# Layer 1's self-attention in a two-layer decoder: values projected by tiles of 128 tokens and moved to batches by DMAs, loads of expert results tied to the steps

## The chip, the cores and the metric

The kernel runs on one core of a Trainium2 chip. A core has five engines with a queue of instructions each: TensorE (PE in the profile, its weight loads PEld), VectorE (DVE), ScalarE (ACT), GpSimd (POOL) and SyncE (SP), which here only issues DMAs. Each queue is worked off in its order. An instruction that needs the result of another queue, or a buffer that another queue still reads, waits at the head of its own queue, and what stands behind it waits too. Matrix products go to PSUM, in eight banks of 128 partitions x 512 floats; the other data lie in SBUF or, outside the core, in HBM. The metric is the time of one execution on the device in microseconds (us).

## What is computed

Two decoder layers over 32 sequences of 100 tokens with 256 features, all in float32. Each layer adds three parts to x, each of the normed x: self-attention, attention to a context of 361 tokens, and a mixture of experts. The part that matters here is the self-attention of layer 1, which has no softmax: scores under the causal mask are used as they are.

```python
def _layernorm(x, axis=-1, eps=1e-05):
    m = jnp.mean(x, axis=axis, keepdims=True)
    v = jnp.var(x, axis=axis, keepdims=True)
    return (x - m) / jnp.sqrt(v + eps)

def _L1_attn_ref(x, W1, b1, W2, b2):
    bs, t, d = x.shape          # 32, 100, 256
    h = N_HEADS                 # 16 heads of 16
    kqv = x @ W1 + b1
    k, q, v = jnp.split(kqv, 3, axis=-1)
    k, q, v = (to_heads(k), to_heads(q), to_heads(v))
    mask = jnp.tril(jnp.ones((t, t), dtype=bool))
    attn = jnp.where(mask, jnp.einsum('bhqd,bhkd->bhqk', q, k), 0.0)
    out = jnp.einsum('bhqk,bhkd->bhqd', attn, v)
    out = out.transpose(0, 2, 1, 3).reshape(bs, t, d)
    return out @ W2 + b2

x = x + _L0_ffn_ref(_layernorm(x), ...)      # two of eight experts for each token
x = x + _L1_attn_ref(_layernorm(x), L1_attn_W1, L1_attn_b1, L1_attn_W2, L1_attn_b2)
x = x + _L1_xattn_ref(_layernorm(x), ctx_512, ...)
```

## The kernel before

x stays in SBUF for the whole program as 25 tiles of 128 tokens (`self.x`, tile f holds tokens 128f to 128f+127 of the 3200), and so does its normed transpose `xnT`. A batch is a sequence of 100 tokens, so a tile cuts across batches: `pieces(b)` lists the parts of tiles that make up batch b, `tile_of(b)` names the tile that batch b completes (or none). The stages follow each other; the one that the change touches is `l1_attn` (1612 to 1785 us of the profiled span), between layer 0's experts (`l0_ffn`) and layer 1's attention to the context.

Layer 0's experts leave their results in HBM (`y_d`), two rows for each token. `gather0(pool, f)` brings them home for tile f: SyncE loads both rows of 128 tokens (L1275, 256 KB, into `yk`, of which there are six buffers), and VectorE adds each, times its weight, to x (L1280, two instructions). After it `norm_stats(f, ...)` takes the mean and variance of the tile on VectorE (L198, L201), and for a group of three tiles (four in the first) the root on ScalarE and its reciprocal. `turn` normalizes the rows of a group (L210), transposes them on TensorE (L232) and copies them to `xnT` (L151 on ScalarE, L152 on VectorE).

The loop runs over steps b = 0 to 33. Step b holds, in the order in which TensorE has it (the order of TensorE is the program's, under `manual_schedule`):

- `scores(b)`: 32 small matmuls for the 16 heads of batch b into four PSUM banks; VectorE multiplies each bank by the mask into SBUF (L1010, four instructions).
- `proj`: queries or keys for one half of the features of the four batches after the present four (four matmuls of 400 columns), to SBUF by ScalarE (L978, L981).
- `vals(b + 1)`: the values of the next batch, four matmuls of 100 tokens x 256 features; VectorE adds the bias into one of three tiles `v0` to `v2` (L991, two instructions). The tiles have 32 columns for each head and hold zeros in the half that the head does not use (even heads use the first 16, odd ones the second), cleared once.
- `values(b - 1)`: 32 small matmuls of masked scores and values (L1020), copied by ScalarE into the transposed tile `zT` (L1027).
- `out(b - 2)`: where that batch completes a tile, the output projection (L157 with `zT`), which VectorE adds to x (L262), and the statistics for the next layer part's norm.
- where there are batches eight ahead: in steps with i = b % 4 < 3 the gather and statistics of one tile of the group two ahead, in the step with i = 3 the turn of that group.
- at times, norm rows and transposes for the next part (GpSimd L210, L1045).

On the other engines the order is made by a scheduler at build time, from the program's order, its own estimate of durations, and dependences; `depend(a, [b], ...)` adds one. In `gather0`, `after` sets VectorE's additions behind the last normalized row. On SyncE the 25 loads `yk` stand in one row, with nothing of this stage between them; a load waits only for its buffer, that is for the additions of the tile six before it.

All tiles of PSUM in this stage share one tag with eight banks, handed out in turn, so the next step's scores need the banks of the present step's scores back.

Of the kernel before, what the change touches and what calls it, by code (L numbers as in the profile page):

```python
# [9 lines left out]
F32 = mybir.dt.float32  # L10
# [3 lines left out]
ALU = mybir.AluOpType  # L14
AX = mybir.AxisListType

P = 128
NB = 32
T = 100
NT = NB * T  # L20
NF = NT // P
D = 256
NK = D // P
H = 16
# [55 lines left out]
def tiles_before(n):  # L80

    return n * T // P


def tile_of(b):

    f = tiles_before(b + 1)
    return f - 1 if f > tiles_before(b) else None


def pieces(b):

    t = 0
    while t < T:
        f, o = divmod(b * T + t, P)
        n = min(P - o, T - t)
        yield f, slice(o, o + n), slice(t, t + n)
        t += n


class Kernel:
# [825 lines left out]
    def l1_attn(self):  # L927
        nc, tc, a = self.nc, self.tc, self.a
        with ExitStack() as st:
            self.psum = st.enter_context(self.banks("l1a", t=8))  # L930
            wk, wq, wv, wo, bqk, bv, bo, xbo = self.w1a
            cp = st.enter_context(tc.tile_pool(name="c1a", bufs=1))
            pool = st.enter_context(tc.tile_pool(name="p1a", bufs=2))
# [7 lines left out]
            at = cp.tile([P, 1], F32, tag="at", name="at")  # L941
# [5 lines left out]
            for j in range(2):  # L947
                got = nc.vector.tensor_scalar(bias[:, j, :], bqk[:, 0, :], own[:, j : j + 1], None, ALU.mult)
                self.depend(got, [self.late.ins], "behind the last block")
            got = nc.vector.tensor_copy(bias[:, 2, :], bqk[:, 2, :])  # L950
            self.depend(got, [self.late.ins], "behind the last block")
            vs = [cp.tile([T, H, 32], F32, tag=f"v{i}", name=f"v{i}") for i in range(3)]
            for v in vs:
                nc.gpsimd.memset(v, 0.0)
            q, k, s, later = {}, {}, {}, deque()
            self.z_begin(pool, 2)

            def group(i):

                f = (0, 3 * i + 1)[i > 0]  # L960
                return range(f, f + FRONT1[f])

            def turn(f, n):
                self.norm_turn(f, n, self.norm_rows(f, n, bias=bo), self.bank_m())

            def proj(b0, i):

                c, of_k = divmod(i, 2)
                if c == 0:
                    if of_k:  # L970
                        k[b0 // 4] = pool.tile([P, 2, 4 * T], F32, tag="kT", name="kT")
                    else:
                        q[b0 // 4] = pool.tile([P, 2, 2, 4 * T], F32, tag="qT", name="qT")
                pm = self.bank_m()[:, : 4 * T]
                w = wk if of_k else wq
                self.mm(pm, [(w[:, i, c * P : (c + 1) * P], self.xn_of(i, b0, 4)) for i in range(NK)])
                if of_k:
                    nc.scalar.activation(k[b0 // 4][:, c, :], pm, AF.Identity, bias=bias[:, 2, c : c + 1])  # L978
                else:
                    for j in range(2):  # L980
                        nc.scalar.activation(  # L981
                            q[b0 // 4][:, c, j, :], pm, AF.Identity, bias=bias[:, j, c : c + 1], scale=own[:, j : j + 1]
                        )

            def vals(b):
                pm = self.bank_m()[:T, :D]
                self.mm(pm, [(self.xn_of(i, b), wv[:, i, :]) for i in range(NK)])
                pv, pb = (t.rearrange("p (h j d) -> p h j d", j=2, d=16) for t in (pm, bv[:T, :]))
                v = vs[b % 3].rearrange("p (h j) e -> p h j e", j=2)
                for j in range(2):  # L990
                    nc.vector.tensor_tensor(  # L991
                        v[:, :, j, 16 * j : 16 * j + 16], pv[:, :, j, :], pb[:, :, j, :], ALU.add
                    )

            def rows_of(r):
                return slice(32 * r, 32 * r + 32)
# [18 lines left out]
            def values(b):  # L1015
                pz = self.bank_z()[:, : 2 * T].rearrange("p (c t) -> p c t", c=2)
                for c in range(2):
                    for j in range(2):
                        for r in range(4):
                            nc.tensor.matmul(  # L1020
                                pz[rows_of(r), c, :], lhsT=vs[b % 3][:, 8 * c + 2 * r + j, :],
                                rhs=s[b, r][:, c, j, :], start=(j == 0), stop=(j == 1),
                            )
                for r in range(4):
                    del s[b, r]
                for z, cols in self.z_parts(b):
                    nc.scalar.copy(z, pz[:, :, cols])  # L1027

            def out(b):

                f = tile_of(b)
                if f is None:
                    return
                self.out_proj(f, wo)
                self.norm_stats(f, HALVES)
                if f in (5, 11, 17):
                    waiting.extend(range(f - 5, f, 2))
# [9 lines left out]

            waiting = deque()


            self.ahead_of = 1

            def ahead(n):
                self.turn_wk1()
                done = []
                for i in range(n):
                    b, half = divmod(i, 2)
                    for c in range(NKC):
                        done.append(self.vals1(b, half, c))
                return done[2 * len(done) // 3]  # L1060

            with tc.manual_schedule(engines={mybir.EngineType.PE}):
                for i in range(2):
                    for f in group(i):
                        if i > 0:
                            self.gather0(pool, f, self.last_row)
                            self.norm_stats(f, FRONT1)
                    if i == 0:
                        self.norm_after = ahead(AHEAD)
                        for f in group(0):  # L1070
                            self.norm_stats(f, FRONT1)
                        self.norm_after = None
                    f = group(i)[0]
                    turn(f, 2)
                    turn(f + 2, len(group(i)) - 2)
                    if i == 0:
                        for c in range(4):
                            proj(0, c)
                vals(0)
                for b in range(NB + 2):  # L1080
                    i = b % 4
                    b0 = b - i
                    if b < NB:
                        scores(b)
                    if b0 + 4 < NB:
                        proj(b0 + 4, i)
                    if b + 1 < NB:
                        vals(b + 1)
                    if 0 < b <= NB:
                        values(b - 1)  # L1090
                    if b > 1:
                        out(b - 2)
                    if b0 + 8 < NB:
                        fs = group(b0 // 4 + 2)
                        if i < 3:
                            self.gather0(pool, fs[i], self.last_row)
                            self.norm_stats(fs[i], FRONT1)
                        else:
                            turn(fs[0], 2)
                            turn(fs[2], 1)  # L1100
                    if later:
                        later.popleft()()
                    if waiting:
                        next_norm()
                while later:
                    later.popleft()()
# [160 lines left out]
                got = nc.sync.dma_start(word, self.y_d[0:1, 0:1])  # L1267
                self.depend(got, [more.ins], "the blocks' results")

    def gather0(self, pool, f, after=None):  # L1270

        nc = self.nc
        pr2 = self.picked0
        y2 = pool.tile([P, 2, D], F32, tag="yk", name="yk", bufs=6)
        got = nc.sync.dma_start(y2, self.y_d.rearrange("(k f p) d -> f p k d", k=2, p=P)[f])  # L1275
        self.depend(got, [self.y_done.ins], "the blocks' results")
        self.tc.declare_no_dep(got.ins, group="y0b", reason="SyncE has waited in the branch")
        for k in range(2):
            y = y2[:, k, :]
            got = nc.vector.scalar_tensor_tensor(  # L1280
                self.x[:, f, :], y, pr2[:, k, f : f + 1], self.x[:, f, :], ALU.mult, ALU.add
            )
            if after is not None:
                self.depend(got, [after.ins], "not ahead of the first tiles' norm")
# [842 lines left out]
```

## Time and profile before

| what | us |
|---|---|
| three timed runs | 2978.18, 2972.26, 2978.78 (median 2978.18) |
| profiled execution | 2953.32 |
| its span, first to last instruction | 2951.6 |
| granted TensorE clock over the span | 0.986 |
| the changed stage in it | about 1612 to 1785 |
| TensorE busy in 1711 to 1785 | 73.85 of 74.00 |
| wait of the loads `yk` for VectorE's additions (their buffers) | 60.9 in 10 waits, longest 19.0 |

A row of the page or of the windows gives busy microseconds and, after an x, instructions. A row of the timeline gives the start, the length, the engine, the line of the kernel, the operation, the tile written and the tiles read, the shapes (partitions x elements), and how many like instructions are merged in it. A float32 product shows as two instructions, so the two halves of a contraction over 256 features make four. Of matmuls in a row, the distance from one start to the next tells more than the length, since they overlap.

### The profile page before, as it was taken

To read this page: it belongs to the slowest core of one execution; us is meant where nothing else is said; L and a number is where in the kernel's file an instruction comes from. 1 tells how busy PE (TensorE), PEld (TensorE's weight loads), DVE (VectorE), ACT (ScalarE), POOL (GpSimd) and SP (SyncE) were. 2 spreads that over 40 slices of the span, in tenths; PEclk is the share of its full clock that TensorE was granted. 3 is DMA by queue.
4 is the path that set the end of the run, shared out by engine and by line. 5 is a ranking of instruction groups with operands and counts; after the bars stand their busy time and mean duration, and the time that the engine had idled before them with its cause. 6 is when DMAs were issued, how large, how long until landed. Compare 5 with 4: busy or idle time off the path is not lost. (4 is left out here: it accounts for less than half of the span.)

```text
span 2951.6 us, 66511 instructions
## 1 busy us (share of the span) xinstructions
PE 2843.2 (96%) x26012; PEld 2165.8 (73%) x26012; DVE 1786.2 (61%) x5119; ACT 1412.2 (48%) x4261; POOL 922.3 (31%) x1081
## 2 busy tenths in 40 slices
PE   8999999999999999999999999999999999999992
PEld 6777777677777766888886667777777777776672
DVE  6665666577777762222225878676676676776553
ACT  5555555467666641222223224565566565667220
POOL 3222221266666536222222230011311212123364
PEclk9999999999999989999999999999999999999997
DMA  8870000000000004565553100010000000000396
GB/s 316 280 263 1 1 1 1 12 15 16 16 16 16 10 28 144 196 221 176 199 214 131 34 2 10 6 42 20 26 12 12 12 12 11 13 10 5 109 214 190
DMA packets 126198, 222.37 MB, mean 75 GB/s; under 512 B 39434, under 2 KB 104645, under 8 KB 119088
## 3 DMA queue, kind: packets, MB, share of 16 engines
q1 hardware_dynamic: 95808, 123.87, 13.1%
q0 software_dynamic: 26784, 90.83, 9.5%
q8 instruction: 210, 3.44, 0.5%
q10 hardware_dynamic: 3280, 3.28, 0.3%
q14 instruction: 116, 0.95, 0.1%
HBM read 152.12 MB, written 111.18 MB: 89 GB/s over the span
## 5 line engine op out<-in xcount | busy, mean ns | idle before, releaser
L1723 POOL DMA_INDIRECT x_d<-xr,slot x200 | 195.2, 976 | 676.4 <-ACT eT L791 548.2
L157 PE MATMUL ps_t<-xnT,wA 128*128 128x200 f32 (+1 forms) x1608 | 329.3, 348 | 0.8 <-DVE x_sb L262 0.6
L157 PE MATMUL ps_t<-cT,q 128*128 128x361 f32 x832 | 317.3, 470 | 0.0
L791 ACT COPY eT<-ps_t 124x384 f32<-124x384 f32 (+1 forms) x416 | 193.6, 473 | 224.6 <-PE ps_t L790 224.3
L781 ACT ACTIVATE wBx<-ps_t,m 128x361 f32<-128x361 f32 x416 | 235.8, 568 | 121.7 <-DVE m L778 117.6
L157 PEld LDWEIGHTS ps_t<-xnT,wA 128*128 128x128 f32 x1608 | 270.2, 190 | 32.0 <-issue 13.2
L540 DVE TENSOR_REDUCE m<-ps_t 100x1 f32<-100x361 f32 x512 | 239.5, 524 | 46.5 <-PE ps_t L157 46.3
L157 PE MATMUL ps_t<-xT,w 128*128 128x256 f32 (+1 forms) x1276 | 260.2, 363 | 0.7 <-ACT xT L151 0.7
L778 DVE TENSOR_REDUCE m<-ps_t 128x1 f32<-128x361 f32 x416 | 218.3, 526 | 60.4 <-PE ps_t L157 58.4
L157 PEld LDWEIGHTS ps_t<-xT,w 128*128 128x128 f32 x1276 | 223.6, 190 | 36.2 <-issue 9.3
L790 PEld LDWEIGHTS ps_t<-ident,wBx 128*124 128x124 f32 x1248 | 156.1, 139 | 123.5 <-issue 68.2
L359 POOL TENSOR_TENSOR e<-e,rz 100x400 f32<-100x400 f32 x128 | 109.3, 854 | 406.4 <-DVE rz L358 402.3
L562 ACT ACTIVATE e<-ps_t 121x300 f32<-121x300 f32 x512 | 173.9, 426 | 119.2 <-PE ps_t L157 119.2
L790 PE MATMUL ps_t<-ident,wBx 128*124 128x128 f32 x1248 | 204.0, 275 | 5.3 <-DVE m L1659 2.1
L355 ACT ACTIVATE e<-s,m 100x100 f32<-100x100 f32 x512 | 186.1, 365 | 20.8 <-DVE m L349 20.1
L157 PE MATMUL ps_t<-wA,cT 128*124 128x512 f32 x384 | 193.9, 592 | 0.0
L783 DVE TENSOR_SCALAR wBx<-wBx,sums 128x361 f32<-128x361 f32 x416 | 173.3, 417 | 9.9
L1377 DVE TENSOR_TENSOR h<-ps_t,g 128x256 f32<-128x256 f32 (+1 forms) x145 | 58.2, 401 | 188.5 <-ACT g L1376 188.5
L157 PEld LDWEIGHTS ps_t<-q,k 32*121 32x121 f32 x3072 | 127.5, 180 | 35.5 <-issue 11.2
L802 PEld LDWEIGHTS ps_t<-eT,v 124*64 124x64 f32 x3072 | 133.0, 137 | 16.4 <-ACT wBx L781 5.1
L1376 ACT ACTIVATE g<-ps_t 128x256 f32<-128x256 f32 (+1 forms) x145 | 52.9, 365 | 190.9 <-PE ps_t L157 190.9
L782 DVE RECIPROCAL sums<-sums 128x1 f32<-128x1 f32 x416 | 66.3, 159 | 125.7 <-ACT wBx L781 124.6
(334 smaller groups left out, 5779.6 us busy)
## 6 DMA issues: line engine op xcount, KB each, us to landing
x_d<-fill SPq DMA_DIRECT2D x16, 1284.0 KB, 22.2
we<-in_wexp SPq DMA_DIRECT2D x32, 384.0 KB, 4.6
cT<-in_ctxT SPq DMA_DIRECT2D x64, 186.0 KB, 2.3
xe_d<-zero SPq DMA_DIRECT2D x8, 1028.0 KB, 15.4
xe<-x_d SPq DMA_DIRECT2D x24, 321.0 KB, 3.9
sum<-fill SPq DMA_DIRECT2D x10, 640.0 KB, 9.0
yk<-y_d SPq DMA_DIRECT2D x25, 256.0 KB, 3.0
xe<-xe_d SPq DMA_DIRECT2D x24, 257.0 KB, 2.6
```

What stands on the lines that cost most here:

```text
L157: self.nc.tensor.matmul(out, lhsT=l, rhs=r, start=(i == 0), stop=(i == n - 1))
L355: nc.scalar.activation(t[:, i, :], s[:, i, :], AF.Exp, bias=m[:, i : i + 1], accum_out=rz[:, i : i + 1])
L359: nc.gpsimd.tensor_tensor(t[:, h, :], t[:, h, :], self.last(rz[:, h], T), ALU.mult)
L540: got = nc.vector.tensor_reduce(m[:, j, o : o + 1], ps[r], AX.X, ALU.max, negate=True)
L562: nc.scalar.activation(t[:, r], ps[r].rearrange("p (c t) -> p c t", c=NKC), AF.Exp)
L778: self.after = nc.vector.tensor_reduce(m, ps, AX.X, ALU.max, negate=True)
L781: nc.scalar.activation(t, ps, AF.Exp, bias=m, accum_out=z)
L783: nc.vector.tensor_scalar(t, t, z, None, ALU.mult)
L790: nc.tensor.transpose(pt[:, c, :], es[n % 5][:, c * KC : (c + 1) * KC], self.ident)
L791: self.after = nc.scalar.copy(eT[:, :, i * P : i * P + w], pt[:, :, :w])
L802: nc.tensor.matmul(pz[64 * j : 64 * j + 64, i, :], lhsT=v[:, c, h * 64 : (h + 1) * 64], rhs=eT[:, c, o : o + T], start=(c == 0), stop=(c = ...
L1723: got = nc.gpsimd.indirect_dma_start(out=self.x1_d[:, :], out_offset=bass.IndirectOffsetOnAxis(ap=slot[:, j, k : k + 1], axis=0), in_=xr[: ...
```

## The change

The values are no longer projected by batches of 100 tokens but by tiles of 128: `vals(f)` takes tile f of `xnT`, VectorE adds the bias into one of two staging tiles `vt0`, `vt1`, and SyncE moves the tile's rows by one DMA for each batch that it touches into that batch's tile `v`, of which there are five, handed out in turn. `value_steps(1, 1, 1)` says which tile is projected in which step: the last tile that still comes in time, that is a tile at least one step before the first batch it touches, one tile in a step at most. Tile 0 is projected ahead of the loop; steps 3, 8, 12, 17, 21, 26 and those from 30 on have none. `made` keeps VectorE's last bias addition of each tile, and the loads of `gather0` in the loop (from step 2 on) get a dependence on the addition three tiles back.

```diff
+def parts(f):
+    for b in range(NB):
+        for g, at, cols in pieces(b):
+            if g == f:
+                yield b, at, cols
+
+def value_steps(per, done, slack):
+    steps, at = {}, per * NB
+    for i in range(per * NF - 1, per * done - 1, -1):
+        b = min(b for b, _, _ in parts(i // per))
+        at = min(at - 1, per * b - slack)
+        steps[at] = i
+    assert at >= 0
+    return steps
...
-            vs = [cp.tile([T, H, 32], F32, tag=f"v{i}", name=f"v{i}") for i in range(3)]
-            for v in vs:
-                nc.gpsimd.memset(v, 0.0)
+            vts = [cp.tile([P, H, 32], F32, tag=f"vt{i}", name=f"vt{i}") for i in range(2)]
+            for t in vts:
+                nc.gpsimd.memset(t, 0.0)
+            v, made = {}, []
...
-            def vals(b):
-                pm = self.bank_m()[:T, :D]
-                self.mm(pm, [(self.xn_of(i, b), wv[:, i, :]) for i in range(NK)])
-                pv, pb = (t.rearrange("p (h j d) -> p h j d", j=2, d=16) for t in (pm, bv[:T, :]))
-                v = vs[b % 3].rearrange("p (h j) e -> p h j e", j=2)
+            def vals(f):
+                pm = self.bank_m()[:, :D]
+                self.mm(pm, [(self.xn_at(i, f), wv[:, i, :]) for i in range(NK)])
+                pv, pb = (t.rearrange("p (h j d) -> p h j d", j=2, d=16) for t in (pm, bv))
+                t = vts[f % 2].rearrange("p (h j) e -> p h j e", j=2)
                 for j in range(2):
-                    nc.vector.tensor_tensor(
-                        v[:, :, j, 16 * j : 16 * j + 16], pv[:, :, j, :], pb[:, :, j, :], ALU.add
+                    got = nc.vector.tensor_tensor(
+                        t[:, :, j, 16 * j : 16 * j + 16], pv[:, :, j, :], pb[:, :, j, :], ALU.add
                     )
+                made.append(got)
+                for b, rows, to in parts(f):
+                    if b not in v:
+                        v[b] = pool.tile([T, H, 32], F32, tag="v", name="v", bufs=5)
+                    nc.sync.dma_start(v[b][to, :, :], vts[f % 2][rows, :, :])
...
-                                pz[rows_of(r), c, :], lhsT=vs[b % 3][:, 8 * c + 2 * r + j, :],
+                                pz[rows_of(r), c, :], lhsT=v[b][:, 8 * c + 2 * r + j, :],
...
+            value_at = value_steps(1, 1, 1)
...
-                    if b + 1 < NB:
-                        vals(b + 1)
+                    if b in value_at:
+                        vals(value_at[b])
...
-                            self.gather0(pool, fs[i], self.last_row)
+                            self.gather0(pool, fs[i], self.last_row, made[-3] if b > 1 else None)
...
-    def gather0(self, pool, f, after=None):
+    def gather0(self, pool, f, after=None, behind=None):
...
         got = nc.sync.dma_start(y2, self.y_d.rearrange("(k f p) d -> f p k d", k=2, p=P)[f])
         self.depend(got, [self.y_done.ins], "the blocks' results")
...
+        if behind is not None:
+            self.depend(got, [behind.ins], "not ahead of the values' moves")
```

## The prediction

> **What bounds the kernel now.** I read the page's busy times first, then the windows over the changed stage (1612 to 1785 us of the span), then TensorE's timeline in it, then the gather's own view. Columns of a window after its length: busy us (and instructions) of PE, PEld, DVE, ACT, POOL, then the clock granted, DMA share, GB/s.
>
> ```profile
> PE 2843.2 (96%) x26012; PEld 2165.8 (73%) x26012; DVE 1786.2 (61%) x5119; ACT 1412.2 (48%) x4261; POOL 922.3 (31%) x1081
> ```
>
> ```profile
> 1634.00:1656.00 22.00, 21.84 (x310) 14.92 (x306) 18.80 (x51) 5.55 (x15) 2.50 (x3) 1.00 0.13 38
> 1656.00:1679.00 23.00, 22.84 (x298) 15.64 (x294) 20.10 (x56) 5.76 (x16) 9.30 (x10) 1.00 0.12 36
> ...
> 1711.00:1785.00 74.00, 73.85 (x1149) 52.21 (x1147) 54.84 (x146) 18.70 (x52) 24.99 (x27) 1.00 0.01 2
> ```
>
> TensorE is full, so an instruction that leaves it shortens the span. But VectorE is at 86% here against 61% over the span (74% in the last part), and the next rows show that it sets the pace in some steps.
>
> ```profile
> 1638.02 1.03 PE L157 MATMUL ps_t<-wB,xnT 128*100 128x256 f32 x4
> 1638.97 0.89 PE L1020 MATMUL ps_t<-s,v 100*32 100x100 f32 x32
> 1639.80 1.13 PE L157 MATMUL ps_t<-wB,zT 128*128 128x256 f32 x4
> 1640.86 1.83 PE L157 MATMUL ps_t<-qT,kT 32*100 32x100 f32 x32
> 1642.62 1.61 PE L157 MATMUL ps_t<-xnT,wB 128*128 128x400 f32 x4
> ...
> 1651.93 0.96 PE L157 MATMUL ps_t<-qT,kT 32*100 32x100 f32 x32
> 1652.83 1.61 PE L157 MATMUL ps_t<-xnT,wB 128*128 128x400 f32 x4
> ```
>
> From start to next start a step is: scores 0.89, projection of queries or keys 1.45, value projection 0.96, values 0.83, together 4.12; the output projection adds 1.06, three norm turns 0.7, two turns for the next layer 0.55. Unhindered scores take 0.89 (the last pair of rows), those at 1640.86 take 1.76: they wait for PSUM banks that VectorE has not emptied. The cause stands just before:
>
> ```profile
> 1636.99 1.04 DVE xn L210 x2
> 1638.06 1.70 DVE x_sb L1280 x2
> 1639.76 1.93 DVE s L1010 x4
> ```
>
> Two gathers' additions go ahead of the masking that TensorE needs. Subtracting the floor of each step from the distance between its values matmuls gives the stalls: 3.94 in step 1 (8.06 between values), 0.87, 0.91, 0.87, 0.91 in steps 4, 5, 8, 9, and 0.25, 0.93, 0.48, 0.88, 0.15 in 12, 13, 16, 17, 20. Together 10.2; after step 20 there is none.
>
> **The change, part by part.**
>
> *Projection.* 25 sets of four matmuls replace 32: 7 x 0.96 = 6.7 us less on TensorE. The output projection has the new shape already (128*128, 128x256): 0.97 to its next start at 1745.94, 1.06 at other places where a wait follows. I take no price for the 128 columns; 25 x 0.09 = 2.3 is the far end. Steps 3, 8, 12, 17, 21, 26, 30 lose their projection.
>
> *Bias addition.* 14 of 64 go; a pair takes 0.40 from start to start, 0.28 each as a row: 7 x 0.40 = 2.8 us less on VectorE. That 128 rather than 100 partitions take part costs nothing: just before the stage L1377 multiplies 128x128 in 0.29 and L1390 64x128 in 0.28.
>
> *Moves.* SP gets 56 new DMAs (the tiles cut at the batches), each 4 to 100 rows of 2 KB. A tile is projected one step before the first batch it touches or earlier, and values reads that batch a step after its scores: two steps, at least 8.2 us. Needed: addition 0.4, up to three issues of 0.36 (the SP rows of the gather), landing. No row shows a move from SBUF to SBUF; the gather's 256 KB bound it, 2.6 to 5.0, below by the copy of 64 KB of the gate (2.4). So 4 to 6.5 us: hidden by 1.7 at worst, and I cost it nothing. Without that cover TensorE would stand in values until the move lands. The moves also wait until values(b-5) has read the tile that they overwrite; that ran at least a step before. The next-but-one addition into a staging tile waits for its moves, two projections back: done. GpSimd clears two tiles instead of three, 0.54 less where it idles.
>
> The rule against it: the Trainium skill, "SBUF — State Buffer", section "The DMA setup-cost knee", puts about 2 us on each transfer whatever its size, plus bytes at 436 GB/s, and asks for few large ones. By it a move of 200 KB is an estimated 2.5 us and a gather 2.6; the gather's row says 3.0 in the middle. By the page the waits below would be 0.4 shorter each.
>
> *Loads of expert results.* This decides.
>
> ```profile
> L1275 SPq DMA_DIRECT2D yk<-y_d x25: 359/360/499, 1591.3 to 1666.9; - x25
> ...
> DMA to landing us min/median/max: 2.6/3.0/5.0
> ```
>
> Before, loads ran up to six tiles ahead (last issue 1666.9, last addition 1710.5), so no addition waited in the loop, and the order of VectorE bunched them. The instruction order of the changed kernel has nine loads issued ahead as before; from tile 9 on, each load stands on SP just behind the moves of one tile of values, and its two additions on VectorE just behind the masking of the following step, one gather to a step. `made[-3]` counts by program order, but the additions stand two steps before their place in the text: the lead is one step, not three. So the bunches go (up to 10.2 us), and a wait comes. Its size: from the end of a bias addition two or three issues of 0.36, then 3.0: 3.8 to 4.2 us to landing; if all landed like the slowest, 6.2. VectorE gets there after values 0.83, scores 0.89 and masking 2.0, less 0.65 from projection to addition's end: 3.1 us, or 4.1 where an output projection lies between. The wait is 0.7 to 1.1, or none (up to 3 at the slow end). Behind it on VectorE stand the next bias addition, the statistics, the output projection's addition, the copy of the turned tiles (which TensorE's next projection needs) and the next masking.
>
> I followed the two queues through steps 0 to 9 by these rows (masking 0.5, gather's addition 0.39, statistics 0.45 with their aggregate, three norm rows 1.3, landing 3.1). Tile 9's addition is reached at 1619.9 and its load lands at 1621.7: 1.8 lost, but scores(3) end at 1628.0 instead of 1630.7. In step 3 the wait is again 1.8; it holds the copy of the turned tiles, so the projection of step 4 starts 2.2 late, and values(3) is 1.3 ahead of before. Step 6 waits 1.4, of which 0.8 reaches step 8. values(9) then starts at 1668.6 instead of 1673.2: 4.6 gained, out of 7.5 stalls and two projections (1.9). Steps 10 to 20: two projections 1.9 and 2.7 of stalls gained, three groups' waits of 0.8 paid: 2.3. Steps 21 to 33: three projections, 2.9. Sum 9.8. One correction: the moves (256 KB a tile) go directly ahead of the load through the same queue. Of the six loads issued back to back the span of landings is 2.6 to 5.0, so a predecessor costs about 0.4; part of it is covered by the issue gap. I take 0.2 more per landing, which reaches TensorE some eight times: 1.6. Forecast 8.2 us less.
>
> The profiled execution took 2953.3 (span 2951.6, 1.7 around it). 2953.3 - 8.2 = 2945.1, 0.28% less. The median of the runs is 2978.2, 0.84% above that execution, and nothing shown tells which stage makes it; the same share off the median gives 2970.
>
> **Rivals.**
>
> *No measurable change* (within 0.2%, 6 us, about what a measurement of this kernel can tell). VectorE becomes the bound. Five steps with four gathers (4 to 8) hold 23.5 us of VectorE (masking 9.75, gathers 4.9, value additions 1.6, output additions 3.2, copy 0.65, norms 3.4) and took 28.15 before. If each gather waits 1.1 in full, 23.5 + 4.4 = 27.9: nothing gained there, and only the last three projections count: 2.9 us, or 2975. For: 86% busy. Against: TensorE runs a step ahead of VectorE, which absorbs part of a wait.
>
> *Slower: the load lands late.* One mechanism, on SP: each load queues behind two or three moves. Break-even is where 23.5 + 4w exceeds 28.15 by what the last part gives (2.9 / 4 per five steps): w = 1.35 mean wait, a landing near 3.8. If they land at 5.0, the slowest seen, the mean wait is near 2.6: 33.9 per five steps, 5.8 lost, four times, less 2.9: 20 us, or 2998. For: the bytes before each load double. Against: a DMA share of 0.13 there.
>
> *The floor:* waits all hidden, 10.2 + 6.7 less 2 for step 1's norm chain: 15 us, 2963. Against it: the wait counted above is longer than the cover in steps without output projection.
>
> *That the change doesn't do what it says* is excluded: the order shows the 25 projections, 56 moves and loads between them.
>
> **How the numbers follow.** Forecast (6 to 14 gained) 0.46; floor 0.10; no change 0.24; slower 0.20. So faster 0.56, same 0.24, slower 0.20. The likeliest case is 2964 to 2972 with 2970 its value. Both signs hold much, so the range reaches past the floor for the spread of the runs (2972 to 2979), to 2959, and halfway up the slow rival, to 2989.
>
> **What would show it.** Right: 100 matmuls of the value projection with 128 columns; scores at 0.89 in what were steps 4, 5, 8, 9; L1280's successor waiting on the load by 0.5 to 1.8 us in about ten steps; the stage 8 us shorter; nothing else moved. Wrong: no wait on the load (the floor), TensorE waiting in values for a move (cover gone), or masking late after each load by 2 us or more (the slow rival). An execution-wide clock other than 0.986 would spoil the comparison, not the argument.

## The result, and the profile after

| | before | after |
|---|---|---|
| median of five runs, us | 2975.95 (2972.26 to 2978.78) | 2991.05 (2989.89 to 2995.99) |
| ratio, 95% interval | 1 | 1.0054 [1.0041, 1.0067] |
| profiled execution, us | 2953.32 | 2991.05 |
| first scores of the stage to the next stage's first matmul, us | 172.90 | 185.56 |
| waits of the gather's additions for their load in the steps, us | none | 24.3 in 13 |

The changed kernel is slower by 0.54%, some 15 us, where 8 less was forecast; 2991 lies 2 us beyond the range. The profiled executions differ by more, 37.7, because the one of before was quick (23 us under its median) and the one of after was not; beside the experiments the kernel before took 2953 or 2954 us on two chips and 2977 on a third. The stage explains 12.7 of them; 12.0 stand ahead of its first scores and 13.1 behind it, nearly all in work that the change does not touch. So everything below is read from the stage, and from ratios against the kernel before on the same chip.

First the page's busy times of after.

```profile
PE 2852.4 (95%) x25984; PEld 2171.8 (73%) x25984; DVE 1783.1 (60%) x5105; ACT 1414.1 (47%) x4261; POOL 922.1 (31%) x1080
```

The removed work is gone: 28 matmul instructions and 14 of VectorE's fewer than before. Then two windows over the part of the stage that had TensorE 99% busy before (columns as above: length, busy PE, PEld, DVE, ACT, POOL, granted clock, DMA share, GB/s).

```profile
1643.80:1665.30 21.50, 18.10 (x235) 12.48 (x234) 11.95 (x34) 4.85 (x13) 0.41 (x1) 0.91 0.18 55
1665.30:1691.60 26.30, 23.03 (x303) 15.51 (x302) 20.57 (x57) 6.05 (x18) 5.21 (x7) 0.94 0.23 64
```

TensorE now stands idle for 3.4 and 3.3 us in them, and in the first of them VectorE is less busy than before too (12.0 of 21.5; it was 18.8 of 22.0). Neither engine bounds this part any more; both wait. For what, the list of waits from 1624 to 1811 us says (total us, times, longest):

```profile
DVE x_sb L1307 <- DMA yk<-y_d: 24.3, 13, 4.1
...
PEld ps_t L176 <- DVE s L1035: 8.4, 22, 1.8
...
PE ps_t L176 <- DVE xnT L171: 7.5, 5, 3.4
PE ps_t L176 <- DVE vt L1011: 4.3, 3, 2.5
PE ps_t L176 <- DVE s L1035: 3.4, 4, 1.7
```

VectorE's one large wait that before did not have is for the loads of expert results (L1307 is the addition that was L1280). TensorE waits for things that VectorE makes behind it: masked scores, the turned tile, the emptied bank. No row has TensorE waiting for a move. Follow one such wait through three timelines, VectorE first (start, length, engine, line, operation, tiles, shapes, how many; in brackets the idle time before it and what ended it):

```profile
1641.24 0.48 DVE L1011 TENSOR_TENSOR vt<-ps_t,wB 128x128 f32<-128x128 f32 x2
...
1642.19 1.98 DVE L1035 TENSOR_TENSOR s<-ps_t,keepT 100x400 f32<-100x400 f32 x4
1648.30 1.00 DVE L1307 SCALAR_TENSOR_TENSOR x_sb<-yk,wA,x_sb 128x256 f32<-128x256 f32 x2 [4.13 <-DMA yk<-y_d]
...
1650.10 0.66 DVE L171 COPY xnT<-ps_t 128x512 f32<-128x512 f32 x1
```

SyncE's queue at the same time:

```profile
1641.75 2.28 SPq L1018 DMA_DIRECT2D v<-vt  x3
1644.07 0.51 SPq L1300 DMA_DIRECT2D yk<-y_d  x1
```

And TensorE:

```profile
1643.82 1.07 PE L1045 MATMUL ps_t<-s,v 100*32 100x100 f32 x32
...
1646.53 0.96 PE L176 MATMUL ps_t<-qT,kT 32*100 32x100 f32 x32
1650.90 1.53 PE L176 MATMUL ps_t<-xnT,wB 128*128 128x400 f32 x2 [3.40 <-DVE xnT L171]
```

The bias addition ends at 1641.72 and releases three moves. They hold SyncE's queue for 2.3 us, so the load is issued at 1644.07, and its data are there at 1648.30, 4.2 us later. VectorE was done with the masking at 1644.17 and stands until then. Behind it in its queue are the statistics, the copy of the turned tile and the next masking; TensorE has run out of work at 1647.5 and gets the turned tile at 1650.9. From these values (1643.82) to the next (1654.97) TensorE took 11.15 us; the same distance was 5.83 before.

Not all of the 5.3 us more is waiting. Three windows, from the end of the scores to the next values:

```profile
1647.50:1650.90 3.40, 0.00 (x1) 0.03 (x1) 2.53 (x7) 0.00 (x0) 0.00 (x0) 1.00 0.00 0
1650.90:1653.55 2.65, 2.65 (x4) 1.34 (x5) 2.27 (x6) 0.00 (x0) 0.00 (x0) 0.53 0.00 0
1653.55:1654.97 1.42, 1.42 (x6) 0.91 (x4) 0.00 (x0) 1.11 (x2) 0.00 (x0) 0.68 0.00 0
```

TensorE is idle for 3.40 us. Then it runs at a granted clock of 0.53 and 0.68: the projection of queries or keys takes 2.65 us instead of 1.45, the value projection 1.42 instead of 0.96. In windows of 0.1 us the clock is 0.50 from 1651.0 to 1654.4. After has four such stretches in the stage, each 3.4 us long and begun less than 2 us after TensorE had waited for VectorE; by the granted clock they cost 1.7 us each, 6.8 together. Before has one, in step 1, from 1624.5 to 1627.9:

```profile
1623.14 2.28 PE L157 MATMUL ps_t<-qT,kT 32*100 32x100 f32 x30 [0.95 <-DVE s L1010]
1625.35 2.87 PE L157 MATMUL ps_t<-xnT,wB 128*128 128x400 f32 x4
1628.06 1.03 PE L157 MATMUL ps_t<-wB,xnT 128*100 128x256 f32 x4
```

So 5.1 of the 12.7 us that the stage became longer are TensorE at half clock, not TensorE waiting.

### The profile page after: what moved, and what is told of

The parts are those of the page before. It is cut to its first block, busy times and chain, and to the rows that moved or that the text cites. A ratio compares the mean times of both kernels' runs of the same rounds, so it can differ in the third digit from the quotient of the medians.

```text
span 2989.3 us, 66573 instructions
## 1 busy us (share of the span) xinstructions
PE 2852.4 (95%) x25984; PEld 2171.8 (73%) x25984; DVE 1783.1 (60%) x5105; ACT 1414.1 (47%) x4261; POOL 922.1 (31%) x1080
## 5 line engine op out<-in xcount | busy, mean ns | idle before, releaser
L821 PE MATMUL ps_t<-eT,v 124*64 124x100 f32 x3072 | 144.1, 252 | 6.8 <-issue 6.6
```

What stands on the lines that cost most here:

```text
L821: nc.tensor.matmul(pz[64 * j : 64 * j + 64, i, :], lhsT=v[:, c, h * 64 : (h + 1) * 64], rhs=eT[:, c, o : o + T], start=(c == 0), stop=(c = ...
```

## The experiments

The stage is measured as in the table above. E1 to e4 ran beside a kernel before of 2952.71 us, e6, e7, e8 and e10 beside one of 2977.48, e11, e12 and e14 beside one of 2954.01 (different chips); each ratio is against its own. Each stage is from one profiled execution. Stages of different chips may be compared: e2 and e10, alike but for the tie and with kernels before that are 25 us apart, have the same stage to 0.01 us. The column at half clock is what the stretches at a granted clock of 0.50 cost in the stage.

| kernel | what it is | stage us | ratio [95%] | waits for loads in the steps, us | half clock, us |
|---|---|---|---|---|---|
| before | | 172.90 | 1 | none | 1.7 |
| after | | 185.56 | 1.0054 [1.0041, 1.0067] | 24.3 in 13 | 6.8 |
| e1_no_tie | loads free | 168.74 | 0.9984 [0.9975, 0.9994] | none | 0 |
| e2_pinned | tie kept, additions held to their own step | 162.46 | 0.9965 [0.9951, 0.998] | none | 1.7 |
| e3_tie_alone | before, with the tie alone | 191.56 | 1.0059 [1.0043, 1.0076] | 34.6 in 16 | 3.4 |
| e4_no_moves | after, without the moves | 175.21 | 1.0015 [1.0005, 1.0025] | 16.9 in 12 | 1.7 |
| e6_moves_pool | e1, moves on GpSimd | 171.14 | 0.9986 [0.9977, 0.9996] | none | 1.7 |
| e7_before_pinned | before, additions held to their step | 162.86 | 0.9978 [0.9967, 0.9989] | none | 0 |
| e8_pinned_pool | loads free, pin, moves on GpSimd | 162.12 | 0.9955 [0.9938, 0.9971] | none | 1.7 |
| e10_pinned_free | loads free, pin, moves on SyncE | 162.47 | 0.997 [0.9958, 0.9983] | none | 1.7 |
| e12_lead_two | tie one tile further back | 184.49 | 1.0036 [1.0024, 1.0049] | 19.4 in 14 | 8.5 |
| e14_pin_masking | e8, pinned to the masking | 159.16 | 0.9945 [0.9929, 0.9962] | none | 0 |
| e11_shifted | e14, skipped steps moved | 158.75 | 0.9941 [0.9924, 0.9958] | none | 0 |

**The tie taken away (e1).**

```diff
-    self.gather0(pool, fs[i], self.last_row, made[-3] if b > 1 else None)
+    self.gather0(pool, fs[i], self.last_row)
```

> The changed kernel with one argument less: the loads of expert results no longer depend on the value additions three tiles back; projection by tiles and moves stay. Theory A (the load lands late: it stands behind two or three moves that take SyncE about 0.8 us each, lands 3 to 4.3 us after its own issue, and VectorE waits 31 us for it in total): the waits for loads fall below 8 us, the stage loses 10 to 20 us, the ratio to the kernel before is 0.994 to 0.999. Rival B (TensorE waits for the moves, not VectorE for the loads): the waits for the moves stay, the ratio stays at 1.003 to 1.007. Rival C (what the tie gives, the additions spread over the steps, is worth more than it costs): ratio above 1.0054.

Without the tie the stage is 16.8 us shorter than after's and 4.2 shorter than before's, and no addition waits for a load. So the loss comes with the tie; projection and moves together are a small gain. Of the 4.2, 1.7 lie in the clock: e1 has before's wait in step 1 (0.96 us), but no stretch at half clock behind it, and no run shows that this repeats.

**The tie alone (e3).** Before, with VectorE's last bias addition of each batch kept in `made` and the load made to depend on `made[-3]`; values by batches, no moves.

```diff
+    got = nc.vector.tensor_tensor(...)   # the bias addition
+    made.append(got)
...
-    self.gather0(pool, fs[i], self.last_row)
+    self.gather0(pool, fs[i], self.last_row, made[-3] if b > 1 else None)
```

> The kernel before with the tie alone: values by batches as before, no moves, but each load depends on the value addition three batches back. Theory A with the weight on the moves: without them a load is issued within 0.4 us of the addition and lands 3 us later, so VectorE waits 0 to 1 us in a step, 0 to 12 us in total, and the bunches go: ratio 0.997 to 1.001. Rival D (the tie by itself is the loss, since it leaves a load one step): waits of 20 us or more and a ratio of 1.004 or above.

A miss of my theory, which put most of the weight on the moves: the tie alone costs as much as the whole change (18.7 us of stage). The view of the tile `yk` in it (issue min/median/max in ns; then VectorE's waits for the loads, those ahead of the steps counted in, and the landing):

```profile
L1277 SPq DMA_DIRECT2D yk<-y_d x25: 359/360/506, 1592.3 to 1751.8; - x25
...
  DMA yk<-y_d: 41.2, 19
...
DMA to landing us min/median/max: 2.6/3.2/5.4
```

Issue and landing are nearly as good as before's (360 ns and 3.0). What differs is the place of the additions on VectorE:

```profile
1655.69 0.48 DVE L992 TENSOR_TENSOR v<-ps_t,wB 100x128 f32<-100x128 f32 x2
1658.91 0.48 DVE L1284 SCALAR_TENSOR_TENSOR x_sb<-yk,wA,x_sb 128x256 f32<-128x256 f32 x1 [2.74 <-DMA yk<-y_d]
1659.32 2.01 DVE L1012 TENSOR_TENSOR s<-ps_t,keepT 100x400 f32<-100x400 f32 x4
```

and on SyncE:

```profile
1656.20 0.36 SPq L1277 DMA_DIRECT2D yk<-y_d  x1
```

The load is issued 0.03 us after the bias addition that releases it, and the gather's addition is the very next instruction of VectorE: a landing of 2.7 us from issue, and no cover for it at all. The masking, which TensorE needs, comes behind it. `made[-3]` reads like three steps of lead, and in VectorE's queue there is none.

**The moves alone taken away (e4).** All batches read one cleared tile `v0`, so the attention's values are left out of the output.

```diff
-    v[b] = pool.tile([T, H, 32], F32, tag="v", name="v", bufs=5)
-    nc.sync.dma_start(v[b][to, :, :], vts[f % 2][rows, :, :])
+    v[b] = v0
```

> The changed kernel without the 56 moves (the values matmuls read one cleared tile, so the attention's values are left out of the output); projection by tiles and the tie stay. Theory A: as in the tie alone, and seven projections less: waits for loads 0 to 12 us, ratio 0.994 to 0.999, that is 16 to 33 us below the changed kernel. Rival D (the tie by itself): waits of 20 us or more remain, ratio 1.000 to 1.005.

10.4 us of the stage go, 5.1 of them because three stretches at half clock fewer follow; the waits fall from 24.3 to 16.9. Free of moves ahead of it, a load is issued in 0.36 us again, but it is still late twelve times. So the loss has two parts: tie and order, and on top of them the moves that stand ahead of each load.

**The additions held to their own step, tie and moves kept (e2).** The scheduler may no longer draw them two steps ahead of their place in the program.

```diff
-    self.gather0(pool, fs[i], self.last_row, made[-3] if b > 1 else None)
+    self.gather0(pool, fs[i], made[-1] if b > 1 else self.last_row, made[-3] if b > 1 else None)
```

> The changed kernel, with the two additions of each gather held behind the newest value addition of their own step, so that they stand two steps later on VectorE while their loads keep their place. Theory A: the load now has 10 us instead of 5, so the waits for loads all but vanish (under 3 us of the 31), and since one gather stands in each step the stalls of before go too: stage 8 to 16 us shorter than before, ratio 0.994 to 0.998. Rival B (TensorE waits for the moves): ratio still above 1.002. Rival C (the cost is the number of instructions on SyncE or the transfers themselves, wherever they stand): ratio 1.003 to 1.007.

No wait for a load is left, and the stage is 23.1 us shorter than after's, 10.4 shorter than before's. The tie costs nothing as soon as VectorE's order gives the load the steps that the program seems to give it. E10 (the same with the loads free) has the same stage to 0.01 us:

```diff
-    self.gather0(pool, fs[i], self.last_row, made[-3] if b > 1 else None)
+    self.gather0(pool, fs[i], made[-1] if b > 1 else self.last_row)
```

> As the pinned kernel (additions in their own step, moves on SyncE) but without the tie, so that loads may go ahead of the moves as far as the six buffers allow. Theory A (the lead is what counts, not the tie): loads are early, ratio as the pinned kernel's, 0.995 to 0.998. Rival G (without the tie a load at the head of SyncE's queue waits for its buffer and holds the moves behind it back): TensorE waits for moves, ratio 0.999 to 1.004.

**The same pin on the kernel before (e7).** Nothing else of the change.

```diff
-    self.gather0(pool, fs[i], self.last_row)
+    self.gather0(pool, fs[i], made[-1] if b > 1 else self.last_row)
```

> The kernel before, values by batches and loads free to run ahead as there, with one dependence more: the two additions of a gather stand behind the newest value addition of their own step, so one gather stands in each step instead of three in a row. Theory A (the 10 us of stalls of before come from the bunches): scores are back at 0.89 us in steps 4, 5, 8, 9; stalls 10.2 to below 4, the stage 5 to 9 us shorter, ratio 0.997 to 0.9985. Rival E (VectorE is simply full in these steps, whatever its order): stalls stay near 10, ratio 0.9995 to 1.001.

The stage loses 10.0 us, 1.7 of them before's stretch at half clock; the stalls that the prediction summed were 10.2. TensorE's timeline in it:

```profile
1666.78 0.89 PE L1022 MATMUL ps_t<-s,v 100*32 100x100 f32 x32
1667.60 1.13 PE L157 MATMUL ps_t<-wB,zT 128*128 128x256 f32 x4
1668.66 0.96 PE L157 MATMUL ps_t<-qT,kT 32*100 32x100 f32 x32
1669.56 1.61 PE L157 MATMUL ps_t<-xnT,wB 128*128 128x400 f32 x4
1671.00 1.03 PE L157 MATMUL ps_t<-wB,xnT 128*100 128x256 f32 x4
1671.96 0.89 PE L1022 MATMUL ps_t<-s,v 100*32 100x100 f32 x32
```

From values to values 5.18, with scores that run through in 0.89 from start to start. That is the floor 4.12 plus an output projection of 1.06, and it holds in what were steps 4, 5, 8 and 9 with 6.05 to 6.09; step 1 goes from 8.06 to 4.12. The bunched additions were the cause of the old stalls (in step 1 with the half clock that followed).

Between e7 and e2 lies the projection by tiles: only 0.4 us of stage instead of 6.7. Seven distances between values lose a projection. Five of them (those from values(1), values(15), values(19), values(24) and values(28)) are 0.86 to 1.03 shorter, 4.5 in all, but the distances that follow the first and the fourth give back 0.7 and 0.4; the other two become longer (5.84 to 6.52 from values(6); 11.9 to 14.2 over the two from values(10)). E2's VectorE within the distance from values(10), which is 8.02 there and 6.30 in e7:

```profile
1676.70 0.47 DVE L1011 TENSOR_TENSOR vt<-ps_t,wB 128x128 f32<-128x128 f32 x2
1677.20 1.61 DVE L1307 SCALAR_TENSOR_TENSOR x_sb<-yk,wA,x_sb 128x256 f32<-128x256 f32 x2
...
1679.19 0.41 DVE L171 COPY xnT<-ps_t 128x256 f32<-128x256 f32 x1
```

and its TensorE:

```profile
1676.51 1.72 PE L176 MATMUL ps_t<-qT,kT 32*100 32x100 f32 x32
1679.74 2.60 PE L176 MATMUL ps_t<-xnT,wB 128*128 128x400 f32 x4 [1.51 <-DVE mv L220]
```

The projection of queries or keys starts 0.14 us after the copy of the turned tile ends. Just after a turn, with the pin's additions ahead of that copy, TensorE now waits for it, here 1.51 us. What follows is again a stretch at half clock (1680.1 to 1683.5, under the projection and the values), for 1.7 us more; e7 has none. Wait and clock are 3.2 of the 3.3 us by which these two distances miss the 0.96 that they should have lost. Without the stretch, the projection by tiles would be worth 2.1 us between e7 and e2.

**Moves on GpSimd (e6: e1 with them; e8: e10 with them).**

```diff
-    nc.sync.dma_start(v[b][to, :, :], vts[f % 2][rows, :, :])
+    nc.gpsimd.dma_start(v[b][to, :, :], vts[f % 2][rows, :, :])
```

> The changed kernel without tie and without pin, moves on GpSimd's queue: against the run without the tie it tells what the moves cost on SyncE when they are shared with loads. Theory A: little, since no load is tied there: ratio 0.997 to 0.999, as without the tie (0.9984). Rival H (the 0.8 us issues on SyncE delay the first values of the stage): ratio 0.994 to 0.9965.

> The changed kernel with the additions pinned to their step, the loads free of the tie, and the 56 moves issued by GpSimd's queue instead of SyncE's, so that no load stands behind a move. Theory A: no wait for a load and no wait for a move, ratio 0.994 to 0.9965, at or a little below the pinned kernel. Rival F (GpSimd, which also normalizes rows for the next part, becomes late, and with it the moves): TensorE waits in values, ratio 0.998 to 1.004.

E6 has the ratio of e1 (0.9986 and 0.9984); its stage is 2.4 us longer, 1.7 of them a stretch at half clock in step 1 that e1 does not have. E8 and e10 have overlapping intervals, and stages 0.35 us apart. Without a load that is due behind them, the moves have no cost on SyncE that these runs can tell.

**The tie one tile further back (e12).**

```diff
-    self.gather0(pool, fs[i], self.last_row, made[-3] if b > 1 else None)
+    self.gather0(pool, fs[i], self.last_row, made[-4] if b > 1 else None)
```

> The changed kernel with one number changed: a load depends on the value addition four tiles back instead of three; nothing is pinned. A load is issued one step earlier against additions that stand where they stood. Theory A (the time between a load's issue and its additions on VectorE is what decides; a step more is 4 to 6 us and the waits were 1.9 each): waits for loads from 24 us in the loop to under 6, ratio 0.997 to 1.000. Rival B (what costs is that loads stand behind moves at all, on the same queue): waits of 12 us or more stay, ratio above 1.002.

A miss: I expected the waits to all but go, and 19.4 of 24.3 us stay, as the rival of the expectation said. VectorE in it:

```profile
1633.21 0.48 DVE L1011 TENSOR_TENSOR vt<-ps_t,wB 128x128 f32<-128x128 f32 x2
...
1634.16 1.98 DVE L1035 TENSOR_TENSOR s<-ps_t,keepT 100x400 f32<-100x400 f32 x4
1640.09 1.00 DVE L1307 SCALAR_TENSOR_TENSOR x_sb<-yk,wA,x_sb 128x256 f32<-128x256 f32 x2 [3.94 <-DMA yk<-y_d]
```

and SyncE:

```profile
1633.72 2.30 SPq L1018 DMA_DIRECT2D v<-vt  x3
1636.06 1.68 SPq L1300 DMA_DIRECT2D yk<-y_d  x1
```

It is the picture of after again: the load stands behind the moves of the newest addition, the gather's additions behind the next masking. The lead is set by the two queues, not by the number in the program.

**Pinned to the masking of the own step (e14), and the skipped steps moved (e11).** In e8 the additions wait for the newest bias addition. In e14 they wait for the masking, so that they come earlier in the step; e11 moves the skipped steps 3, 8 and 12 to 6, 10 and 14, away from the turns.

```diff
-    self.gather0(pool, fs[i], made[-1] if b > 1 else self.last_row)
+    self.gather0(pool, fs[i], self.masked if b > 1 else self.last_row)
...
+    for skip, to in ((3, 6), (8, 10), (12, 14)):      # e11 only
+        for n in range(skip, to):
+            value_at[n] = value_at.pop(n + 1)
```

> The pinned kernel with its moves on GpSimd's queue, pinned to the masking of its own step instead of the value addition, so the additions stand a little earlier in the step, also in steps without a projection. It is the base for the next run. Theory A: as that kernel, ratio 0.994 to 0.997. Rival: they again stand ahead of the value addition and the copy of the turned tiles, and hold those back: 0.997 to 0.999.

> As the run pinned to the masking, with three of the seven steps without a projection moved: 6, 10 and 14 instead of 3, 8 and 12, that is away from the turn of a group, after which TensorE's next projection waits for VectorE's copy. Theory A (a step without projection after a turn gains nothing, since its 0.96 us only covered that wait; elsewhere it gains 0.9): 1.5 to 2.7 us less than the run pinned to the masking, ratio 0.0005 to 0.001 lower. Rival I (the seven projections are lost time in any place, because VectorE sets the pace of the whole group): no difference between the two, within 0.8 us in the stage.

Both beat both kernels: 0.9945 and 0.9941. E14 gains 3.7 us of stage over e7: the distance from values(6) is now 4.98, the one from values(10) 4.76, and no stretch at half clock is left. That is over half of the projection's 6.7, but the order differs from e7's as well; a kernel by batches pinned to the masking was not run, so what of the 3.7 is the projection's and what the order's is not shown. E11 gains 0.4 more, where I had expected 1.5 to 2.7; the rival, no difference within 0.8, fits. The distances from values(4), values(8) and values(12) lose a projection and become 4.32. Those that get theirs back grow: the one from values(1) by 0.9, about the projection, but those from values(6) and values(10) by 1.3 and 2.0. Why these two grow by more is not settled.

## Why the prediction was wrong

- **The step that failed is the wait in "Loads of expert results".** The place was right: lead of one step and not three, loads behind the moves of one tile, additions behind the next masking. Its size was not: "the wait is 0.7 to 1.1, or none" became 1.9 in the mean (24.3 in 13) and up to 4.1. It is beyond the 1.35 that the prediction itself gave as break-even. With it goes a term that the sum does not have: the clock of TensorE behind a wait.
- *The cover.* I reckoned 3.1 to 4.1 us on VectorE from the addition's end to the gather's addition, from the rows of an engine kept busy by TensorE. In the example it is 2.45 (1641.72 to 1644.17). Once VectorE is late, the scores that it masks are long done, and values and scores on TensorE no longer lie between. With the tie alone there was none: the gather's addition is VectorE's next instruction (e3). A late engine loses its cover, and so stays late.
- *Issue and landing.* I priced a move's issue by that of the loads, 0.36; it took 0.53 to 1.20, in the middle 0.755. In the example load and moves took 6.6 us from the addition's end (1641.72 to 1648.30), where 3.8 to 4.2 was said: 2.3 until the load's issue for some 1.1, then 4.2 to the data for 3.0. Leaving the moves out saved 10.4 us (e4).
- *The step-by-step sum through the queues* counted on TensorE, a step ahead, to absorb part of each wait. It absorbed little: 185.56 less the stage's floor (172.90 - 10.2 - 6.7 = 156.0) leaves 29.6 us, of which 6.8 are the half clock and 22.8 stalls, for 24.3 of waits. The prediction gave back 8.7 of its possible 16.9.
- *The clock* has no term in the sum; the prediction only says that a clock other than 0.986 over the execution would spoil the comparison. It was 0.982 over the execution, and in the stage four stretches at 0.50 cost 6.8 us where before had one. They came with the waits: 5.1 of the 12.7 us that the stage lost.
- *The stalls of before* (10.2, from bunched additions) were read rightly in their sum: e7 removes 10.0 with the pin alone. But 1.7 of the 3.94 in step 1 were TensorE at half clock, which the windows shown, from 1634 on, do not contain.
- *The projection's 6.7 us* are right as TensorE's work, and the seven steps are the ones named. As time on the path they are wrong: 0.4 (e2 against e7; 2.1 without e2's stretch at half clock) to at most 3.7 (e14 against e7, where the order differs too), since a shorter TensorE next to a turn waits for VectorE's copy.
- *The moves hidden behind two steps* held for those who read them: TensorE never waited for one. What I missed is that they are not free for the load behind them.
- *Rivals.* "Slower: the load lands late" came true, priced at 20 us and measured at 15. But its mechanism, the place behind two or three moves, is only a part of it. That the tie and VectorE's order suffice without a single move (e3) was not among the rivals.

## What to carry to other kernels

Count a load's lead in the queues: from the instruction that releases it to the instruction that needs it, on the engine that executes both, as the scheduler has placed them; a count of program steps says nothing where the consumer may be drawn ahead. If you throttle a load, hold its consumer back as well, or the throttle becomes a wait with all that stands behind it. And the cover that an engine has while it keeps pace is not the cover that it has once it is late. Read the granted clock of the stage, too, before calling every lost microsecond a wait: here a wait of TensorE cost up to 1.7 us beyond its own length.

## What the runs showed of the hardware

The issue of a move from SBUF to SBUF took twice as long on SyncE as that of a 256 KB load, and its spread was large; the loads between them were also issued more slowly (0.473 in the middle, 0.360 before). Two rows from the views of the tiles in after (ns, min/median/max):

```profile
L1018 SPq DMA_DIRECT2D v<-vt x56: 532/755/1197, 1626.9 to 1802.6; - x56
...
L1300 SPq DMA_DIRECT2D yk<-y_d x25: 359/473/1199, 1600.7 to 1750.2; - x25
```

On GpSimd the same moves take less, and land in 2.6 us in the middle, where the loads of that kernel take 3.3 (e14):

```profile
L1018 POOL DMA_DIRECT2D v<-vt x56: 505/537/675, 1618.3 to 1766.9; - x56
...
DMA to landing us min/median/max: 1.7/2.6/5.1
```

A load alone in its queue had its data in 2.7 us from issue (e3, 1656.20 to 1658.91), behind three moves in 4.2 (after) and 4.0 (e12). The Trainium skill, "SBUF — State Buffer", section "The DMA setup-cost knee", gives a transfer about 2 us and its bytes at 436 GB/s, an estimated 2.6 for a load of 256 KB: the lone load agrees, the one behind moves took 1.6 more, which that rule for one transfer does not contain. Whether those 1.6 lie in the transfer engines or in the queue was not tried.

The clock granted to TensorE in this stage stood at 1.00 or at 0.50. The stretches at 0.50 that were read finely (four in after, one each in before and e2) were 3.4 us long, and each began 0.1 to 1.8 us after TensorE had waited. Not every wait brings one: behind the same wait in step 1 (0.95 and 0.96 us) before has a stretch and e1 has none.
